# Sums of a graph layer moved to idle buffers, one accumulator made known to a planned order, and the planned lengths set anew

## The chip, the cores and the metric

One core of a Trainium2 chip runs the whole program. The metric is the device time in microseconds (us) of that core; lower is better. PE stands for TensorE (matmuls), DVE for VectorE, ACT for ScalarE, POOL for GpSimd, SP for SyncE, which here issues nearly all DMAs.

## What is computed

The input is x (3327 x 256) and a dense matrix adj (3327 x 3327), of whose entries about 0.5% and the diagonal are not zero. Two layers follow each other, both with a layer norm and a ReLU ahead and a residual after. Layer 0 takes two steps over the graph and over a learned sparse attention; layer 1 attends over the neighbours with four heads.

```python
R = S + eye(N); R = R / R.sum(-1, keepdims=True)        # S is adj
for n in range(2):
    A = top_p_attention(Xa, W1, W2, W3)                 # softmax row, cut to the largest that hold 0.9 of it
    Xf = R @ Xf
    Xa = A @ Xa
    Z = Z + Xf @ U1[n].T + Xa @ U2[n].T
...
e = leaky_relu(s[:, :, None] + d[:, None, :], 0.2)      # layer 1, per head
attn = softmax(where(adj > 0, e, -inf), axis=2)
out = elu(attn @ hp)
```

## The kernel before, in words

N is cut into 26 tiles of 128 nodes (NT = 26, P = 128). All matmuls are float32, each of which the profile shows as two entries.

*How the work is ordered.* The program isn't written in the order in which it runs. Each piece of work is put on record with `plan.put(engine, length, rank, fn, needs=, take=, give=, lag=, hold=)`: the engine, how long the writer thinks it takes (us), a rank, what must be done before, and which named tokens (buffers) it takes and gives back. `Plan.order()` then plays the whole program through with these lengths: whenever an engine is free it takes the ready piece of lowest rank whose tokens are free. `hold` marks a DVE piece as one that stops POOL meanwhile. `plan.issue()` emits the instructions in that order. On the chip every engine runs its own instructions strictly in the order so found, and semaphores see to the true dependences. A length that is off therefore never makes a wrong result; it makes an order that doesn't suit. The tokens exist only in the planner: real buffers are tiles of pools, and a tile that is still in use makes the engine wait whether the planner knew or not.

*Layer 0* has two steps, n = 0 (about 100 to 900 us) and n = 1 (about 900 to 1708 us). In each, 26 rows of three kinds of work interleave:

- Search, per row tile: logits on PE (L882), exponentials on ACT (L893), then a threshold found by rounds: ACT counts over all 3327 columns (L930), POOL (lines 943 to 976; in the last round DVE) works out the next threshold from the count. DVE then takes windows (L985, L990), sorts, chooses, and drops the entries under the threshold (L1042).
- Attention, per row tile: PE transposes the row in groups of four (L1055), ACT copies each group from PSUM (L1060, tiles `et`), PE multiplies (L1067, into `acca`).
- The product with adj, per row tile (class `Full`): SP loads seven pieces of adj (L1088, tiles `at`), PE does 26 matmuls (L1099, into `accf`), ACT copies the result (L1106), DVE adds (L1115, L1121). In step 0 a row's result has its own `accf` tile of 257 columns. In step 1 one tile of [128, 2, 256] serves all rows, and rows use its two halves in turn; the planner has a token for each half (`accf0`, `accf1`).

*Layer 1* (`attend_neighbours`, 1708 to 2177 us) goes over four blocks of 832 target nodes, and in each over 26 source tiles j: a mask from adj on ACT (L1634, L1635), the exponents on DVE in two halves of two heads each (L1646, into an `e` tile of [128, 4, 832]), the product on PE in two halves (L1662), and for every second j the denominators on PE (L1676). The `e` tiles are seven in turn: for j % 7 < 4 one of four tiles of the pool `e` (token "e"), else one of three made from large tiles that layer 0 has left (token "e2"). When a block is done, its sums leave PSUM: ACT copies the numerators (L1724) and the denominators (L1727) to an SBUF tile, which is also one of the pool `e`. From that, for each 128 targets, PE transposes three times (L1746), DVE inverts (L1750), ACT forms both parts of elu (L1758), DVE joins and adds x (L1762, L1763), SP stores. This runs during the next block.

*The verdict.* The fast way holds for inputs in a certain reach. At the end a flag says whether it held: five small DVE operations, then twice a DVE copy, a PE transpose (L1936) and a DVE maximum (L1937), and a last DVE operation (L1938). All engines load the flag and branch past the general way (L1945). These instructions stand after `plan.issue` in the text.

Of the kernel before, what the change touches and what calls it, by code (L numbers as in the profile page):

```python
# [19 lines left out]
P = 128  # L20
# [552 lines left out]
def fast(  # L573
# [59 lines left out]
    with ExitStack() as l0:  # L633
# [215 lines left out]
        plan = Plan(dict(rows=1, mvs=3, pl=2, px=2, acca=1, accf=1, accf0=1, accf1=1, et=3, at=4, y=1, e2=3, mask=2, **BUFS))  # L849
# [227 lines left out]
        class Full:  # L1077


            def __init__(self, n, t):  # L1080
                self.n, self.t, self.at = n, t, {}
                self.src, self.w = (main, D + 1) if n == 0 else (c, D)
                self.bank = f"accf{t % 2}" if n else "accf"
# [6 lines left out]
            def some(self, js):  # L1090
                for j in js:
                    if j == 0 and self.n == 0:
                        self.acc = ps_a.tile([P, D + 1], F32, name="accf")
                    elif j == 0:

                        if self.t == 0:
                            late["accf"] = ps_a.tile([P, 2, D], F32, name="accf")
                        self.acc = late["accf"][:, self.t % 2, :]
                    T.matmul(  # L1099
                        self.acc[:, : self.w], self.at[j // JC][:, j % JC, :], self.src[:, j, : self.w],  # L1100
                        start=(j == 0), stop=(j == NT - 1),
                    )
# [30 lines left out]
        def deviations(lo, hi):  # L1133


            m, held = hi - lo, {}

            def first(k):
                if k == 0:
                    held["mv"] = small.tile([P, 4, 4], F32, name="mvs", bufs=3)  # L1140
                st = small.tile([P, V.BN_STATS_DIM], F32, name="bst", bufs=3)
                V.bn_stats(st, rhs[0][:, lo + k, :])
                V.bn_aggr(held["mv"][:, k, :2], st)

            def rest():
                mv = held["mv"][:, :m]
                GP.tensor_scalar(mv[:, :, 2], mv[:, :, 1], LN_EPS, None, ALU.add)
                GP.tensor_tensor(mv[:, :, 2], mv[:, :, 2], powers[:, 0:1].to_broadcast([P, m]), ALU.pow)
                GP.tensor_tensor(mv[:, :, 3], mv[:, :, 0], mv[:, :, 2], ALU.mult)
                GP.tensor_scalar(mv[:, :, 3], mv[:, :, 3], -1.0, None, ALU.mult)  # L1150

            a = []
            for k in range(m):
                a.append(
                    plan.put("DVE", 0.62, -100.0 + lo + k, first, k, needs=[loads[lo + k], a], take=["mvs"] * (k == 0))
                )
            a = plan.put("POOL", 1.1 + 0.2 * m, -100.0 + lo, rest, needs=[a])
            return {lo + k: (a, held, k, k == m - 1) for k in range(m)}

        def prepare(t, measured):  # L1160
# [36 lines left out]
            a = hs[0][t] = plan.put("ACT", 0.6, r, relu, needs=[ready_], give=["mvs"] * last)  # L1197
            a = plan.put("PE", 0.25, r, turn, needs=[a], take=["pl"])
            a = turned_h[t] = plan.put("DVE", 0.43, r, copy, needs=[a], give=["pl"])
            a = plan.put("PE", 0.5, r, project, needs=[a, weighed], take=["px"])  # L1200
            a = plan.put("ACT", 0.3, r, share, needs=[a], take=["kq"], give=["px"])
# [9 lines left out]
        def project_u(t, rank):  # L1211
            held = {}


            bank = ("acca", "accf")[t % 2] if t > 7 else "px"

            def product():
                ps = held["ps"] = (ps_x if bank == "px" else ps_a).tile([P, 2 * D], F32, name=bank)
                for k in range(2):
                    T.matmul(ps, c[:, t, k * P : (k + 1) * P], u1[:, k, :], start=(k == 0), stop=(k == 1))  # L1220

            a = plan.put("PE", 1.75, rank, product, needs=[turned_h[t], uloads], take=[bank])
            b = plan.put("ACT", 0.37, -2.3, lambda: S.copy(main[:, t, :D], held["ps"][:, :D]), needs=[a])
            e = plan.put("DVE", 0.43, -2.3, lambda: V.tensor_copy(c[:, t, :], held["ps"][:, D:]), needs=[a])
            plan.put("SP", 0.0, -2.6, lambda: None, needs=[b, e], give=[bank], lag=0.0)
            return b, e
# [91 lines left out]
        def finish2(row, done, z, rank):  # L1318
# [67 lines left out]
            a = plan.put("POOL", 0.85, r, deviation, False, needs=[a])  # L1386
            a = plan.put("DVE", 1.6, r, second, needs=[a, x_], take=["mv"], give=["mv"], hold=0.95)
            s_ = plan.put("SP", 0.1, r, store, needs=[a])
            a = plan.put("POOL", 1.1, r, deviation, True, needs=[a])
# [6 lines left out]
            return plan.put("DVE", 0.6, r, scale, needs=[a], give=["f"]), s_  # L1396
# [24 lines left out]
        def search(row, rank, keys, stats_of, fresh):  # L1421
# [4 lines left out]
            for g in range(2):  # L1426

                def logits(g=g):
# [4 lines left out]
                    "PE", 2.0 - 0.8 * g, rank - 2.5, logits, needs=[keys, fresh, a], take=["pl", "pl"] + ["e", "sc"] * (1 - g)  # L1433
# [8 lines left out]
            a = row.pieces["guess"] = plan.put("ACT", 1.0, rank - 2.4, row.guess, needs=[a])  # L1442
            more = plan.put("ACT", 0.85, rank - 2.2, row.density, needs=[a])
# [6 lines left out]
            if EVALS[n] == 3:  # L1450
                a = row.pieces["counted"] = plan.put("ACT", 3.05, rank - 1.4, row.count, 2, AF.Sign, needs=[a])
                a = plan.put("DVE", 2.7, rank - 1.3, row.step, 2, V, needs=[a])
            halves = []
            for h in range(2):
                for part in range(2):
                    a = plan.put(
                        "DVE", 3.2 - 2.0 * part, rank - 1.0, row.window, h, part, needs=[a], take=["y"] * (1 - part),
# [8 lines left out]
            for o in range(4):  # L1466
                a = plan.put("DVE", 1.03, rank - 1.0, row.drop, o, needs=[a], hold=1.0)
                drops.append(a)
# [4 lines left out]
        def attention(row, rank, total, drops, right):  # L1473
            a = None
            for g in range(GROUPS):
# [6 lines left out]
                b = plan.put("ACT", 0.03 + 0.115 * m, rank - 2.6, row.turned, g, needs=[b], take=["et"], give=["px"])  # L1482
# [5 lines left out]
        def full(n, t, rank, right, after):  # L1488
# [7 lines left out]
            for j in range(0, NT, 2):  # L1496
# [3 lines left out]
                    take=[f.bank] * (j == 0) + ["accf"] * (n == 1 and t + j == 0), give=["at"] * last,  # L1500
                )
            a = plan.put(
                "ACT", 0.3, -90.0, f.copy, needs=[a], take=["f"],
                give=[f.bank] + ["accf"] * (n == 1 and t == NT - 1),
# [6 lines left out]
        def attend_neighbours(rows, ends, done, fulls):  # L1511
# [78 lines left out]
            for b in range(4):  # L1590
# [14 lines left out]
                for j in range(NT):  # L1605
# [83 lines left out]
                    else:  # L1689
# [7 lines left out]
                        "DVE", 2.1, rank, exponents, 0, needs=[m_, both[0], ends[j][0], more if mine == "e2" else None,  # L1697
                        logits_done, last_e], take=[mine], hold=2.0,
                    )
                    y_ = plan.put("DVE", 2.1, rank, exponents, 1, needs=[x_, both[1]], give=own, hold=2.0)  # L1700
# [8 lines left out]
                    if len(group) == JG or j == NT - 1:  # L1709
                        for n_, (fn, name) in enumerate(group):  # L1710
                            last_den = plan.put(
                                "PE", 1.42 + 0.2 * (n_ == 0), rank, fn, needs=[last_acc, last_den],
# [7 lines left out]
                def leave(k, q=q):  # L1720
                    if k == 0:
                        q["ot"] = epool.tile([P, NP], F32, name="e")[:, : 3 * W].rearrange("p (k c w) -> p k c w", k=3, c=2)
                    if k < 2:
                        S.copy(q["ot"][:, k], q["acc"][k][:, :, :C])  # L1724
                    else:
                        for c in range(2):
                            S.copy(q["ot"][:, 2, c], q["den"][c][:, :C])  # L1727

                r1 = r0 + 9.0
                first = plan.put("ACT", 0.9, r1, leave, 0, needs=[last_acc], take=["e"], give=["pl"])  # L1730
# [3 lines left out]
                for x0 in range(0, W, P):  # L1734
# [7 lines left out]
                    def turn(m=m, x0=x0, q=q, held=held):  # L1742
                        held["pr"] = ps_x.tile([P, 3, P], F32, name="px")
                        ot = q["ot"].rearrange("p k c w -> p k (c w)")
                        for k in range(3):
                            T.transpose(held["pr"][:m, k, :], ot[:, k, x0 : x0 + m], ident)  # L1746
# [63 lines left out]
                    elif x0 % (4 * P) == 0:  # L1810
                        f_ = plan.put("SP", 0.4, r1, fetch_all, needs=[used_heads[0] if x0 == 0 else [last_e, f_], touched], take=["e"] * (x0 > 0), lag=4.0)
                    a = plan.put(
                        "PE", 0.4, r1 + 0.02, turn, needs=[out_of], take=["px"], give=["e"] * (x0 + P >= W)
# [9 lines left out]
                    a = plan.put("ACT", 2.0, r1, elu, needs=[a], take=["ystage"], give=["px", "mv"])  # L1823
                    a = plan.put("DVE", 1.0, r1, add, needs=[a, f_], give=["f"], hold=0.9)
# [31 lines left out]
        for n in range(STEPS):  # L1856
# [24 lines left out]
            failed.append(plan.put("DVE", 2.2, base + NT, failures, n, needs=[[a for a, _ in found]]))  # L1881
# [41 lines left out]
        plan.issue(tc)  # L1923

        V.tensor_reduce(far, sd.rearrange("p k t h -> p k (t h)"), AX.X, ALU.max, apply_absolute_value=True)
        V.tensor_tensor(far[:, 0:1], far[:, 0:1], far[:, 1:2], ALU.max)
        V.tensor_scalar(far[:, 0:1], far[:, 0:1], REACH, 0.0, ALU.is_le, ALU.is_equal)
        V.tensor_reduce(far[:, 1:2], bad.rearrange("p n t -> p (n t)"), AX.X, ALU.max)
        V.scalar_tensor_tensor(far[:, 0:1], far[:, 1:2], 0.0, far[:, 0:1], ALU.is_gt, ALU.max)

        verdict = const.tile([1, 2], F32, name="verdict")
        for k in range(2):
            r = small.tile([P, D], F32, name="xa", bufs=BUFS["xa"])
            V.tensor_copy(r[:, :1], far[:, 0:1])
            pr = ps_x.tile([1, P], F32, name="px")
            T.transpose(pr, r[:, :1], ident)  # L1936
            V.tensor_reduce(verdict[:, k : k + 1], pr, AX.X, ALU.max)  # L1937
        V.tensor_tensor(again, verdict[:, 0:1], verdict[:, 1:2], ALU.max)  # L1938
# [46 lines left out]
```

## Time and profile before

| what | us |
|---|---|
| median of 3 runs | 2197.55 (2196.28 to 2198.43) |
| the profiled execution | 2193.86 |
| its span in the profile | 2192.1 |
| PE busy in it | 2158.7 |
| DVE busy | 1605.3 |
| ACT busy | 1441.6 |
| POOL busy | 926.6 |
| granted TensorE clock | 0.997 of full |

The page cuts the span in 40 slices of 54.8 us: slices 1 and 2 are the start, about 3 to 16 step 0, 17 to 31 step 1, 32 to 40 layer 1. A digit is the busy share of a slice in tenths. "Busy" of an engine counts the time from an instruction's start to its end; for PE these ends are modelled. The kinds of work that hold PE longest:

| line | what | entries | mean ns of one | busy us |
|---|---|---|---|---|
| L1067 | attention, layer 0 | 2704 | 379 | 618.2 |
| L1099 | product with adj, step 1 | 1352 | 383 | 316.1 |
| L1099 | product with adj, step 0 | 1352 | 381 | 309.8 |
| L1662 | product, layer 1 (one of its groups) | 1024 | 517 | 192.5 |

The entries overlap in time: the mean of one is longer than the step from one start to the next.

### The profile page before, as it was taken

How to read it: one execution, taken by the hardware profiler on the slowest of the kernel's cores; microseconds unless marked ns; L12 is line 12 of the kernel's file. 1: busy time of each engine (PE TensorE's matmuls, PEld its weight loads, DVE VectorE, ACT ScalarE, POOL GpSimd, SP SyncE). 2: the span in 40 equal slices, each digit the busy share in tenths (PEclk: the TensorE clock that was granted, in tenths of full speed). 3: DMA queues.
4: the chain of work that ended last, by engine and by line, in shares of the span. 5: the costliest groups of instructions: out<-in, count | busy, mean ns of one | idle time of the engine just before them, and what ended most of it. 6: DMA issues, size and time to landing. Idle time of an engine off the chain costs nothing. (4 is left out here: it accounts for less than half of the span.)

```text
span 2192.1 us, 35711 instructions
## 1 busy us (share of the span) xinstructions
PE 2158.7 (98%) x11872; PEld 1519.1 (69%) x11872; DVE 1605.3 (73%) x4205; ACT 1441.6 (66%) x2714; POOL 926.6 (42%) x2259
## 2 busy tenths in 40 slices
PE   8999999999999999999999999999999999999997
PEld 6578778778787788777778777878788433333332
DVE  5567666657556571367998888788878898989896
ACT  5786776667666742578888787788673556465553
POOL 5466565546533550265666665656563100000001
PEclk9999999999999999999999999999999999999999
DMA  4012122222222233532222222222124534444341
GB/s 121 21 36 85 48 63 62 64 72 64 57 58 62 72 116 92 154 95 58 63 59 64 59 74 61 75 75 69 56 72 136 157 114 145 119 137 127 110 127 53
DMA packets 192323, 183.74 MB, mean 84 GB/s; under 512 B 15386, under 2 KB 146176, under 8 KB 192128
## 3 DMA queue, kind: packets, MB, share of 16 engines
q1 hardware_dynamic: 191232, 181.15, 28.4%
q8 instruction: 95, 1.56, 0.3%
q14 instruction: 100, 0.82, 0.1%
q10 hardware_dynamic: 896, 0.21, 0.0%
HBM read 164.41 MB, written 15.94 MB: 82 GB/s over the span
## 5 line engine op out<-in xcount | busy, mean ns | idle before, releaser
L1067 PE MATMUL acca<-rhs,et 128*128 128x256 f32 x2704 | 618.2, 379 | 0.1
L930 ACT ACTIVATE junk<-e,sc 128x3327 fp8e5<-128x3327 f32 x182 | 558.8, 3070 | 81.4 <-POOL sc L975 81.0
L1067 PEld LDWEIGHTS acca<-rhs,et 128*128 128x128 f32 x2704 | 498.3, 190 | 61.8 <-issue 1.8
L1099 PE MATMUL accf<-c,at 128*128 128x256 f32 x1352 | 316.1, 383 | 6.3 <-ACT f L1106 5.7
L985 DVE SCALAR_TENSOR_TENSOR y<-e,sc 128x1664 f32<-128x1664 f32 x104 | 204.8, 1969 | 152.6 <-POOL sc L972 150.3
L1099 PE MATMUL accf<-main,at 128*128 128x257 f32 x1352 | 309.8, 381 | 1.5 <-ACT f L1106 1.5
L1099 PEld LDWEIGHTS accf<-c,at 128*128 128x128 f32 x1352 | 249.2, 190 | 54.1 <-issue 10.6
L1099 PEld LDWEIGHTS accf<-main,at 128*128 128x128 f32 x1352 | 251.4, 190 | 46.1 <-issue 8.1
L1060 ACT COPY et<-px 128x512 f32<-128x512 f32 (+1 forms) x364 | 192.6, 553 | 119.5 <-PE acca L1067 62.9
L990 DVE MAX8 cands<-y 128x8 f32<-128x208 f32 x832 | 242.2, 361 | 3.6
L1042 DVE SCALAR_TENSOR_TENSOR e<-e,thr 128x832 f32<-128x832 f32 x208 | 212.9, 1081 | 2.0
L893 ACT ACTIVATE e<-pl 128x1024 f32<-128x1024 f32 x208 | 179.9, 869 | 43.3 <-PE pl L882 43.3
L1635 ACT ACTIVATE et<-at 128x448 bf16<-128x448 f32 (+1 forms) x204 | 112.3, 550 | 131.9 <-DVE e L1646 74.2
L1798 POOL TENSOR_TENSOR qq<-qq 128x256 f32<-128x256 f32 x4 | 3.0, 757 | 461.2 <-ACT qq L1794 461.1
L1055 PE MATMUL px<-ident,e 128*128 128x128 f32 x1352 | 191.9, 274 | 6.0 <-ACT et L1060 3.5
L1055 PEld LDWEIGHTS px<-ident,e 128*128 128x128 f32 x1352 | 160.1, 141 | 50.0 <-issue 13.5
L1662 PE MATMUL pl<-e,main 128*64 128x416 f32 x1024 | 192.5, 517 | 0.3
L882 PE MATMUL pl<-kt,qq 64*128 64x512 f32 (+1 forms) x832 | 173.7, 536 | 0.8 <-ACT e L893 0.8
L1662 PEld LDWEIGHTS pl<-e,main 128*64 128x64 f32 x1024 | 70.9, 137 | 113.3 <-issue 86.4
L1646 DVE SCALAR_TENSOR_TENSOR e<-c,low,et 128x832 f32<-128x832 f32 x128 | 128.6, 1070 | 12.0 <-PE accf L1676 10.4
L882 PEld LDWEIGHTS pl<-kt,qq 64*128 64x128 f32 x832 | 71.5, 186 | 84.4 <-issue 77.3
L1646 DVE SCALAR_TENSOR_TENSOR e<-qq,low,et 128x832 f32<-128x832 f32 x120 | 120.4, 1072 | 6.0 <-PE accf L1676 4.4
(534 smaller groups left out, 3032.3 us busy)
## 6 DMA issues: line engine op xcount, KB each, us to landing
at<-in_adjt_dram SPq DMA_DIRECT2D x414, 256.0 KB
at<-in_adjt_dram SPq DMA_DIRECT2D x102, 192.0 KB
at<-in_adjt_dram SPq DMA_DIRECT2D x52, 128.0 KB
ys<-ystage SPq DMA_DIRECT2D x26, 256.0 KB
rhs<-in_x_dram SPq DMA_DIRECT2D x26, 128.0 KB
ystage<-in_x_dram SPq DMA_DIRECT2D x26, 128.0 KB
base<-ys SPq DMA_DIRECT2D x26, 128.0 KB
x1s<-ystage SPq DMA_DIRECT2D x26, 128.0 KB
```

The source lines that it names most:

```text
L882: T.matmul(pl[:, lo : lo + m], qq[half, self.i, :], kt[half, 512 * k : 512 * k + m], start=True, stop=True,)
L893: S.activation(self.e[:, 1024 * k : 1024 * k + pl.shape[1]], pl, AF.Exp, accum_out=(self.p0, self.p1, self.p2, self.p3)[k],)
L930: S.activation(junk[:, :N], self.e[:, :N], fn, bias=t, scale=-1.0, accum_out=dst, saturate=False)
L985: V.scalar_tensor_tensor(self.y[:, : hi - lo], self.e[:, lo:hi], self.up, self.e[:, lo:hi], ALU.is_lt, ALU.mult, accum_out=(self.h0, self. ...
L990: V.max(self.cands[:, o // PIECE, :], self.y[:, o - lo : min(o + PIECE, hi) - lo])
L1042: V.scalar_tensor_tensor(piece, piece, self.thr[:, o : o + 1], piece, ALU.is_gt, ALU.mult)
L1055: T.transpose(pt[:, k, :], self.e[:, j * P : (j + 1) * P], ident)
L1060: S.copy(self.et[g][:, :m, :], self.pt.pop(g)[:, :m, :])
L1067: T.matmul(self.acc, et[:, j - 4 * g, :], rhs[self.n][:, j, :], start=(j == 0), stop=(j == NT - 1))
L1099: T.matmul(self.acc[:, : self.w], self.at[j // JC][:, j % JC, :], self.src[:, j, : self.w], start=(j == 0), stop=(j == NT - 1),)
L1646: V.scalar_tensor_tensor(held["e"][:, k, :], extra["both"][b % 2][:, k, :], low[:, j, k : k + 1], held["mask"], ALU.max, ALU.mult,)
L1662: T.matmul(q["acc"][a][k * FH : (k + 1) * FH, c, :C], main[:, j, h * FH : (h + 1) * FH], held["e"][:, h, c * C : (c + 1) * C], start=(j == 0),
```

## The change

It has four parts.

(a) The sums of a layer-1 block are copied to a tile `y` (the window tile of layer 0's search, without use in layer 1) and, for the denominators, to the tile `kt` (keys of layer 0), instead of a tile of the pool `e`. The token follows: "y" instead of "e".

(b) In step 1, too, each row has its own `accf` tile, of 256 columns; the pool holds one. The tokens `accf0` and `accf1` are gone: a row's first pair of matmuls takes "accf", its copy gives it back.

(c) Lengths given to the planner are set anew in some thirty places. They add no instruction; they alter the order of the pieces on all engines.

(d) The verdict becomes three planned pieces of rank 92, which lies in the last quarter of layer 1, with one transpose instead of two.

```diff
-        plan = Plan(dict(rows=1, mvs=3, pl=2, px=2, acca=1, accf=1, accf0=1, accf1=1, et=3, at=4, y=1, e2=3, mask=2, **BUFS))
+        plan = Plan(dict(rows=1, mvs=3, pl=2, px=2, acca=1, accf=1, et=3, at=4, y=1, e2=3, mask=2, **BUFS))
...
-                    if j == 0 and self.n == 0:
-                        self.acc = ps_a.tile([P, D + 1], F32, name="accf")
-                    elif j == 0:
-
-                        if self.t == 0:
-                            late["accf"] = ps_a.tile([P, 2, D], F32, name="accf")
-                        self.acc = late["accf"][:, self.t % 2, :]
+                    if j == 0:
+                        self.acc = ps_a.tile([P, self.w], F32, name="accf")
...
-            return plan.put("DVE", 0.6, r, scale, needs=[a], give=["f"]), s_
+            return plan.put("DVE", 0.47, r, scale, needs=[a], give=["f"]), s_
...
-            a = row.pieces["guess"] = plan.put("ACT", 1.0, rank - 2.4, row.guess, needs=[a])
-            more = plan.put("ACT", 0.85, rank - 2.2, row.density, needs=[a])
+            a = row.pieces["guess"] = plan.put("ACT", 1.46, rank - 2.4, row.guess, needs=[a])
+            more = plan.put("ACT", 0.55, rank - 2.2, row.density, needs=[a])
...
-                a = plan.put("DVE", 2.7, rank - 1.3, row.step, 2, V, needs=[a])
+                a = plan.put("DVE", 3.35, rank - 1.3, row.step, 2, V, needs=[a])
...
-                    take=[f.bank] * (j == 0) + ["accf"] * (n == 1 and t + j == 0), give=["at"] * last,
+                    take=["accf"] * (j == 0), give=["at"] * last,
                 )
             a = plan.put(
-                "ACT", 0.3, -90.0, f.copy, needs=[a], take=["f"],
-                give=[f.bank] + ["accf"] * (n == 1 and t == NT - 1),
+                "ACT", 0.35, -90.0, f.copy, needs=[a], take=["f"], give=["accf"],
             )
...
-                        "DVE", 2.1, rank, exponents, 0, needs=[m_, both[0], ends[j][0], more if mine == "e2" else None,
-                        logits_done, last_e], take=[mine], hold=2.0,
+                        "DVE", 2.0, rank, exponents, 0, needs=[m_, both[0], ends[j][0], more if mine == "e2" else None,
+                        logits_done, last_e], take=[mine], hold=1.95,
...
-                        q["ot"] = epool.tile([P, NP], F32, name="e")[:, : 3 * W].rearrange("p (k c w) -> p k c w", k=3, c=2)
+                        q["ot"] = scr.tile([P, 2 * W], F32, name="y").rearrange("p (k w) -> p k w", k=2)
+                        q["ot"] = [q["ot"][:, 0], q["ot"][:, 1]]
                     if k < 2:
-                        S.copy(q["ot"][:, k], q["acc"][k][:, :, :C])
+                        S.copy(q["ot"][k].rearrange("p (c w) -> p c w", c=2), q["acc"][k][:, :, :C])
                     else:
+                        if "den" not in extra:
+                            extra["den"] = wpool.tile([P, 2 * W], F32, name="kt")[:, :W]
+                        q["ot"].append(extra["den"])
                         for c in range(2):
-                            S.copy(q["ot"][:, 2, c], q["den"][c][:, :C])
+                            S.copy(q["ot"][2][:, c * C : (c + 1) * C], q["den"][c][:, :C])
...
-                first = plan.put("ACT", 0.9, r1, leave, 0, needs=[last_acc], take=["e"], give=["pl"])
+                first = plan.put("ACT", 0.9, r1, leave, 0, needs=[last_acc], take=["y"], give=["pl"])
...
-                        "PE", 0.4, r1 + 0.02, turn, needs=[out_of], take=["px"], give=["e"] * (x0 + P >= W)
+                        "PE", 0.4, r1 + 0.02, turn, needs=[out_of], take=["px"], give=["y"] * (x0 + P >= W)
...
-                    a = plan.put("ACT", 2.0, r1, elu, needs=[a], take=["ystage"], give=["px", "mv"])
-                    a = plan.put("DVE", 1.0, r1, add, needs=[a, f_], give=["f"], hold=0.9)
+                    a = plan.put("ACT", 1.6, r1, elu, needs=[a], take=["ystage"], give=["px", "mv"])
+                    a = plan.put("DVE", 0.8, r1, add, needs=[a, f_], give=["f"], hold=0.9)
...
+        verdict = const.tile([1, 2], F32, name="verdict")
+        def judge():
+            V.tensor_reduce(far, sd.rearrange("p k t h -> p k (t h)"), AX.X, ALU.max, apply_absolute_value=True)
...
+        def gather_rows():
+            late["pr"] = ps_x.tile([1, P], F32, name="px")
+            T.transpose(late["pr"], far[:, 0:1], ident)
+        def tell():
+            V.tensor_reduce(verdict[:, 0:1], late["pr"], AX.X, ALU.max)
+            V.tensor_tensor(again, verdict[:, 0:1], verdict[:, 0:1], ALU.max)
+        a = plan.put("DVE", 1.5, 92.0, judge, needs=[[a for a, _ in ends], failed])
+        a = plan.put("PE", 0.15, 92.1, gather_rows, needs=[a], take=["px"])
+        plan.put("DVE", 0.45, 92.2, tell, needs=[a], give=["px"])
         plan.issue(tc)
...
-        for k in range(2):
-            r = small.tile([P, D], F32, name="xa", bufs=BUFS["xa"])
-            V.tensor_copy(r[:, :1], far[:, 0:1])
-            pr = ps_x.tile([1, P], F32, name="px")
-            T.transpose(pr, r[:, :1], ident)
-            V.tensor_reduce(verdict[:, k : k + 1], pr, AX.X, ALU.max)
-        V.tensor_tensor(again, verdict[:, 0:1], verdict[:, 1:2], ALU.max)
```

## The prediction

> **What bounds the kernel now.** I read, in this order, the page's busy times and slices, the list of waits by engine, the timeline at the places that the waits name, and the order of each engine's instructions before and after.
>
> ```profile
> PE 2158.7 (98%) x11872; PEld 1519.1 (69%) x11872; DVE 1605.3 (73%) x4205; ACT 1441.6 (66%) x2714; POOL 926.6 (42%) x2259
> PE   8999999999999999999999999999999999999997
> DVE  5567666657556571367998888788878898989896
> ```
>
> TensorE (PE) is the bound in every stage, and the change leaves its work as it is: the matmuls of the same lines have the same counts in both programs, except for one transpose less at the end. So the most that can be won is the time in which PE stands still. Outside of its first 60 us, PE's visible gaps (times between the end of one entry and the start of the next) sum to 3.5 us in step 0 of layer 0, 11.2 us in step 1 (900 to 1708 us) and under 0.4 us in layer 1. The waits say what those are:
>
> ```profile
> PE accf L1099 <- ACT f L1106: 7.2, 13, 1.1
> ...
> PE px L1055 <- ACT et L1060: 3.5, 2, 3.2
> ...
> PE px L1055 <- DVE e L1042: 1.1, 3, 0.6
> ```
>
> The columns are total us, times, longest. The first line is what part (b) aims at. The timeline around one case (start, length, what; the wait in brackets):
>
> ```profile
> 938.84 0.37 ACT L1106 COPY f<-accf 128x256 f32<-128x256 f32 x1 [2.49 <-PE accf L1099]
> ...
> 939.27 1.99 PE L1099 MATMUL accf<-c,at 128*128 128x256 f32 x8 [0.46 <-ACT f L1106]
> ```
>
> PE went from row t to row t+1 without a pause and did its first 8 matmuls, since row t+1 has its own half of the tile. The copy of row t began only after those (ACT stood idle 2.49 us for PE), and PE then waited for the copy. The start-to-start step of these matmuls is 215 ns; here it is 840, and the step after it 320. There are seven such places, and two with 956: 7 x (0.625 + 0.104) + 2 x (0.741 + 0.104) = 6.8 us; with the gap of 1.1 at the first row (917.6), about 8 us.
>
> Layer 1 looks full on PE and is not. VectorE (DVE) shows waits there:
>
> ```profile
> DVE e L1646 <- PE accf L1676: 14.7, 4, 4.4
> ...
> DVE e L1646 <- ACT e L1724: 3.3, 2, 1.7
> ```
>
> ```profile
> 1853.25 3.01 PE L1662 MATMUL pl<-rhs,main 128*64 128x416 f32 x16
> 1856.10 4.17 PE L1662 MATMUL pl<-e,main 128*64 128x416 f32 x16
> 1860.19 0.91 PE L1676 MATMUL acca<-rhs,qd 128*32 128x416 f32 x8
> ...
> 1863.12 1.27 PE L1662 MATMUL pl<-e,main 128*64 128x416 f32 x6
> ```
>
> The same 16 matmuls took 3.01 us and then 4.17. From 1856.10 to 1863.12 is 7.02 us; the same stretch (product of one j, then its pair's products and sums) takes 5.82 elsewhere. The other two boundaries between column blocks give 7.05 and 7.46. So 1.20 + 1.23 + 1.64 = 4.1 us is lost there, counted as busy. The cause stands 30 us earlier: the sums of a finished block sit in an e tile (line 1724), so the exponents at j=2 and j=3 of the new block wait for a buffer, 18 us in all, so 6.0 per boundary. At j=7 DVE is then 0.5 to 0.9 us behind PE, where it is some us ahead in the rest of a block (DVE needs 3.98 us a j, PE 4.33).
>
> **What the Trainium skill says.** "PSUM — Partial Sum Buffer", Terms: a bank is 2 KiB per partition, and two engines must not be in one bank and quadrant together. Two halves of 256 float32 fill just one bank, so a second half cannot give overlap; the trace agrees with the 2.49 us above. "Trainium Kernel Development and Optimization", Performance Expectations: matmul busy time is a bad measure because matmuls are pipelined; the 4.17 against 3.01 us is this. "TensorE: Matmul & The Clock Gate", Architectural detail: ACT and DVE take their queues strictly in order; the trace agrees in the third rival below. "TensorEngine Tiling (Array Packing)", Key Properties: a change of tiling mode drains TensorE; here the step from L1662 to L1676 is 442 ns against 345, so about 0.1 us a switch.
>
> **The change part by part**, against the profiled execution of 2193.86 us (span 2192.1), which lies 3.69 under the median 2197.55. I carry the difference over to the median.
>
> *Sums to other buffers (a).* The copies of the sums (L1724, L1727) go to the window tile and the old key tile, idle in layer 1. Same copies, same sizes, no DMA. The buffer wait of DVE goes, and in the new DVE order j=0 to j=3 follow each other directly, with the block's epilogue (7 groups of some 1.07 us) from j=4. DVE gets those 6.0 us per boundary back, more than the 0.5 to 0.9 it lacks at j=7. Next late would be DVE itself, but it gains 0.35 us per j. Bounds: -4.1 (all), -1.5 (the epilogue, now in one run, takes the lead back at two boundaries). I take -3.7.
>
> *Accumulator known to the plan (b).* A row change now needs the copy before its first matmul. The plan knows that and can put other PE work there. With nothing there, the wait is about 0.85 us instead of 0.215 (a lone change at the first rows shows 842 ns), so 0.64 + 0.10 = 0.74, the same as a stall now. In the new PE order, three row changes of step 1 are bare (rows 27, 35, 37; nine were before), and five have 0.87 to 1.06 us of cover, the others more. Cover of 1 us hides a copy of 0.37 plus two hand-overs if ACT is free; if a count (L930, 3.07 us) is in front, up to 3 us show. I reckon 3 x 0.74 = 2.2, plus 0.3 at each of ten others at which ACT will be busy, an estimate (a tenth of a count), = 3.0. That is 5.2 instead of 6.8; the 1.1 at the first row stays: -1.6. Bounds: -6 (all covered), +1 (ACT late at more of them).
>
> *Lengths (c).* They add no instruction; they move the order on all engines, and with it each row's DMA issue on SP (`at` loads) and POOL's steps. By the start-to-start steps that are longer than usual, step 1 has 6.7 us of stalls outside the accumulator: 3.4 at 1566.5, 0.8 for one load at 1183, the rest small. Longer plan lengths for guess and the DVE step say later what was in truth later. I take -1.0, bounds -4 and +3 (from nearly none left, to one more like 1566.5). Step 0 and the start: 0, bounds -1 and +1; the trace shows no stall there above 1.1.
>
> *Start of layer 1.* One product piece (4 x 345 ns = 1.4 us) has moved ahead of the last row's adjacency work. It filled the time in which the exponents of j=2 and 3 come after the last row: now PE reaches the second half of j=3 just 0.14 us after DVE (1721.62 against 1721.48). The chain from the last row through copy, finish and four exponents is not shortened. So 1.4 - 0.1 = +1.3; bounds 0 and +1.5.
>
> *Verdict (d).* In PE's order one 128-wide transpose now sits in block 3: 0.11 + two mode switches of 0.1 = +0.3. DVE's pieces (1.5 + 0.45 as planned) stand in front of exponents, but in a block where DVE leads by more than that; if that lead were gone they would cost 2. At the end two transposes and their reductions go. The chain there is this:
>
> ```profile
> 2185.16 0.73 SPq L1805 DMA_DIRECT2D out_dram<-e  x2
> 2185.39 0.27 DVE L1937 TENSOR_REDUCE verdict<-px 1x1 f32<-1x128 f32 x1
> 2185.70 0.15 DVE L1938 TENSOR_TENSOR again<-verdict 1x1 int32<-1x1 f32 x1
> ```
>
> SP issues its last store until 2185.89, the verdict is ready at 2185.85: two chains end together, only one is shortened. I take -0.2; bounds 0 and -0.6.
>
> Sum: -3.7 - 1.6 - 1.0 + 1.3 + 0.3 - 0.2 = -4.9. The profiled execution would be 2189.0, the median 2192.65, said as 2192.7.
>
> **The rivals.** A difference under 0.2% (4.4 us: 2193.15 to 2201.95) is about what a measurement of this kernel cannot tell from none.
>
> *Step 1 is cleaned up as a whole.* The stalls of step 1 are 6.8 + 1.1 + 6.7 = 14.6 us; my sum takes 2.6 of it. If a plan with true lengths removes half, 7.3, the median is 2197.55 - 4.9 - 4.7 = 2188.0. For it: six fewer bare row changes, and each stall comes from an order that was planned with lengths off by up to 0.65 us. Against: the waits for POOL come from steps whose lengths (3.8 and 4.7) were not changed.
>
> *The wait only moves.* Row changes now wait openly for ACT, which is in a count 3 us long for much of the time; step 1 gains nothing, and only half of the boundaries' gain comes (-2.1), less 1.3 + 0.3 - 0.2: -0.7, so 2196.8. For it: ACT is busy 7 to 8 tenths in most slices of step 1. The weaker form, that the change does not do what it says, belongs here: the sums leave the e tiles but the exponents wait for the sums' matmuls (L1676) of the buffers they reuse.
>
> *Slower.* ACT runs in order. The plan may put a count ahead of the copies that PE needs, when its POOL step is late:
>
> ```profile
> 1562.85 3.07 ACT L930 ACTIVATE junk<-e,sc 128x3327 fp8e5<-128x3327 f32 x1 [5.39 <-POOL sc L975]
> ...
> 1566.53 1.09 PE L1055 MATMUL px<-ident,e 128*128 128x128 f32 x8 [3.23 <-ACT et L1060]
> ```
>
> The count waited 5.39 us for POOL, the copies (L1060) stood behind it, PE stood 3.23. Each such place costs 3.2. It happens once now; two more would eat my gain, three make it slower: -4.9 + 3 x 3.2 = +4.7, so 2202.3. For it: the whole order is new, and POOL's lengths are not retuned. Against: once in 52 rows now.
>
> **How the numbers follow.** My sum 2192.7 (own range 2189.5 to 2196): 0.46, of which 0.25 under 2193.15. Step 1 cleaned up, 2188.0: 0.23. The wait moves, 2196.8: 0.17. Slower, 2202.3: 0.14. So faster 0.25 + 0.23 = 0.48, within 0.21 + 0.17 = 0.38, slower 0.14. The range 2186.5 to 2199 leaves out the slower case and the far end of the cleaned-up one.
>
> **What would show it.** Right: no DVE wait for PE at L1639 (the exponents' line after) at a block's j=2 and 3, and 5.8 us stretches at j=7; the wait of L1099 for the copy at 4 to 6 us, before a row's first matmul; a PE gap of about 1 us some 13 us after the last adjacency row. Wrong: waits at L1099 above 8 us, more than one PE gap of 3 us behind a count, or the 7 us stretches still there.

## The result and the profile after

| | us |
|---|---|
| before, median of 12 runs | 2197.49 (2195.89 to 2198.89) |
| after, median of 12 runs | 2198.52 (2196.15 to 2200.91) |
| ratio after to before | 1.0005, 95% interval 0.9997 to 1.0012 |
| forecast | 2192.7 (2186.5 to 2199.0) |
| profiled execution after, and its span | 2199.53, 2197.6 |

The change makes no difference that can be measured, where 4.9 us less were forecast. The measured time lies inside the stated range, 0.5 us from its upper end. The profiled execution of before (2193.86) was a fast one by chance: all of its timed runs lie above it, by 0.7 us or more over the whole study. So the two spans, 5.5 us apart, exaggerate; what follows is read by stage.

The table cuts each profile at four points of PE's work: the first product with adj of step 0, the first of step 1, the first product of block 1 of layer 1, and the last product. The "last product" is the start of its last entry. Two programs that are equal up to a point differ there only by chance.

| profile | start | step 0 | step 1 and block 0 | blocks 1 to 3 | rest |
|---|---|---|---|---|---|
| before | 95.4 | 822.2 | 905.9 | 350.0 | 18.5 |
| after | 98.6 | 824.2 | 910.2 | 346.0 | 18.6 |

Blocks 1 to 3 won 4.0 us. Step 1 with block 0 lost 4.3, step 0 lost 2.0, of which an estimated 1.7 come from a stretch of half clock (last section). The start's 3.2 us aren't the change's: in the profiles of the twelve experiments it took 96.5 to 99.2 us, in six of them with the order of before there.

The page and the waits of after (PE's first, then DVE's in layer 1), whose L1093 is before's L1099, L1100 is L1106, L1639 is L1646, L1655 is L1662, L1669 is L1676:

```profile
PE 2160.0 (98%) x11871; PEld 1520.6 (69%) x11871; DVE 1607.1 (73%) x4202; ACT 1442.7 (66%) x2714; POOL 935.7 (43%) x2259
DVE  5566676547565572277979879788878799999895
```

```profile
PE accf L1093 <- ACT f L1100: 8.6, 11, 2.0
...
PE px L1055 <- ACT et L1060: 2.7, 3, 1.6
PE acca L1067 <- ACT et L1060: 2.2, 2, 2.0
PE px L1232 <- ACT xa L1073: 2.0, 1, 2.0
...
PE px L1055 <- DVE e L1042: 0.8, 2, 0.5
```

```profile
DVE e L1639 <- PE accf L1669: 2.9, 2, 2.2
```

The reader is to see two things. DVE's wait for a buffer fell from 14.7 to 2.9 us. And PE's waits for ACT didn't fall, but changed their places: the accumulator's line grew from 7.2 to 8.6, and two lines are new (L1067 for a copy, L1232 for `xa`).

What was won, at j=7 of block 1 (timeline of PE in after):

```profile
1862.51 3.01 PE L1655 MATMUL pl<-rhs,main 128*64 128x416 f32 x16
1865.36 2.96 PE L1655 MATMUL pl<-e,main 128*64 128x416 f32 x16
1868.25 0.91 PE L1669 MATMUL acca<-rhs,qd 128*32 128x416 f32 x8
...
1871.18 2.32 PE L1655 MATMUL pl<-e,main 128*64 128x416 f32 x12
```

The sixteen matmuls that took 4.17 us take 2.96, and the stretch is 1871.18 - 1865.36 = 5.82 us instead of 7.02.

What was lost. A row change in step 1 (ACT and PE in after): the copy stands behind a count, the count behind POOL, and PE's first matmul of the row behind the copy.

```profile
1204.92 3.07 ACT L930 ACTIVATE junk<-e,sc 128x3327 fp8e5<-128x3327 f32 x1 [2.15 <-POOL sc L975]
...
1207.98 0.35 ACT L1100 COPY f<-accf 128x256 f32<-128x256 f32 x1
...
1208.39 2.86 PE L1093 MATMUL accf<-c,at 128*128 128x256 f32 x12 [1.44 <-ACT f L1100]
```

The end of layer 0 (SP, ACT and PE in after): ACT has the first mask of layer 1 (into `kt`) ahead of the last copy of an attention row. The mask waits 4.59 us for its load, and PE 2.00 us for the copy behind it.

```profile
1665.16 5.78 SPq L1604 DMA_DIRECT2D kt<-in_adjt_dram  x4
...
1673.88 0.90 ACT L1611 ACTIVATE kt<-kt 128x832 f32<-128x832 f32 x1 [4.59 <-DMA kt<-in_adjt_dram]
...
1675.61 0.35 ACT L1060 COPY et<-px 128x256 f32<-128x256 f32 x1
...
1676.01 1.13 PE L1067 MATMUL acca<-rhs,et 128*128 128x256 f32 x4 [2.00 <-ACT et L1060]
```

And the start of layer 1 (PE in after): 32 entries, for which twice the 2.85 us from start to start of 16 would be 5.7 us, take 7.18 us, since DVE's exponents for j=2 and j=3 come late.

```profile
1724.83 7.18 PE L1655 MATMUL pl<-e,main 128*64 128x416 f32 x32
```

### The profile page after: what moved, and what is told of

Same layout as the page of the kernel before. It is cut to its first block, busy times and chain, and to the rows that moved or that the text cites. A ratio compares the mean times of both kernels' runs of the same rounds, so it can differ in the third digit from the quotient of the medians.

```text
span 2197.6 us, 35753 instructions
## 1 busy us (share of the span) xinstructions
PE 2160.0 (98%) x11871; PEld 1520.6 (69%) x11871; DVE 1607.1 (73%) x4202; ACT 1442.7 (66%) x2714; POOL 935.7 (43%) x2259
## 4 chain that ended last, share of the span: by engine, by line
PE 42%; POOL 5%; ACT 4%; issue 1%; DVE 1%; DMA 0%; SPq 0%; DVEq 0%; POOLq 0%; ACTq 0%
PE pl L1655 13%; PE accf L1093 8%; PE acca L1067 8%; PE acca L1669 4%; PE accf L1669 3%; ACT junk L930 3%; PE px L1055 2%; PE pl L882 2%; POOL sc L943 1%; PE px L1359 1%; PE px L1742 0%; POOL sc L968 0%; DMA kt<-in_adjt_dram 0%; DVE e L1639 0%; ACT et L1060 0%
## 5 line engine op out<-in xcount | busy, mean ns | idle before, releaser
L1067 PE MATMUL acca<-rhs,et 128*128 128x256 f32 x2704 | 618.4, 379 | 2.3 <-ACT et L1060 2.2
L1067 PEld LDWEIGHTS acca<-rhs,et 128*128 128x128 f32 x2704 | 498.2, 190 | 66.0 <-ACT et L1060 3.5
L1093 PE MATMUL accf<-c,at 128*128 128x256 f32 x1352 | 315.2, 382 | 7.9 <-ACT f L1100 7.9
L1093 PE MATMUL accf<-main,at 128*128 128x257 f32 x1352 | 309.5, 380 | 0.7 <-ACT f L1100 0.7
L1093 PEld LDWEIGHTS accf<-c,at 128*128 128x128 f32 x1352 | 249.5, 190 | 53.4 <-ACT f L1100 12.6
L1093 PEld LDWEIGHTS accf<-main,at 128*128 128x128 f32 x1352 | 251.6, 190 | 44.3 <-issue 8.3
L1055 PE MATMUL px<-ident,e 128*128 128x128 f32 x1352 | 191.7, 274 | 3.8 <-ACT et L1060 2.7
L1055 PEld LDWEIGHTS px<-ident,e 128*128 128x128 f32 x1352 | 160.0, 141 | 46.8 <-issue 10.9
L1655 PE MATMUL pl<-e,main 128*64 128x416 f32 x1024 | 190.3, 517 | 0.1
L1655 PEld LDWEIGHTS pl<-e,main 128*64 128x64 f32 x1024 | 70.6, 137 | 110.7 <-issue 90.8
L1639 DVE SCALAR_TENSOR_TENSOR e<-c,low,et 128x832 f32<-128x832 f32 x128 | 128.7, 1071 | 5.7 <-issue 3.2
L1627 ACT ACTIVATE at<-at 128x448 f32<-128x448 f32 (+1 forms) x204 | 110.4, 541 | 31.0 <-DMA at<-in_adjt_dram 30.8
```

The costliest lines, as they stand in the source:

```text
L1055: T.transpose(pt[:, k, :], self.e[:, j * P : (j + 1) * P], ident)
L1067: T.matmul(self.acc, et[:, j - 4 * g, :], rhs[self.n][:, j, :], start=(j == 0), stop=(j == NT - 1))
L1093: T.matmul(self.acc[:, : self.w], self.at[j // JC][:, j % JC, :], self.src[:, j, : self.w], start=(j == 0), stop=(j == NT - 1),)
L1655: T.matmul(q["acc"][a][k * FH : (k + 1) * FH, c, :C], main[:, j, h * FH : (h + 1) * FH], held["e"][:, h, c * C : (c + 1) * C], start=(j == 0),
```

## The experiments

Each kernel was timed in five rounds beside the kernel before, whose medians in the three groups were 2197.38, 2197.45 and 2197.79. The theory at the outset: (a) is worth its 4 us, and the new order of layer 0 gives them back. The rival: what the parts bring adds up, and the two profiles differ by chance.

**Each part alone.** `a_sums_only`: the diff's part (a), nothing else.

```diff
-                        q["ot"] = epool.tile([P, NP], F32, name="e")[:, : 3 * W].rearrange("p (k c w) -> p k c w", k=3, c=2)
+                        q["ot"] = scr.tile([P, 2 * W], F32, name="y").rearrange("p (k w) -> p k w", k=2)
...
+                            extra["den"] = wpool.tile([P, 2 * W], F32, name="kt")[:, :W]
...
-                first = plan.put("ACT", 0.9, r1, leave, 0, needs=[last_acc], take=["e"], give=["pl"])
+                first = plan.put("ACT", 0.9, r1, leave, 0, needs=[last_acc], take=["y"], give=["pl"])
```

> The kernel before with part (a) alone: the sums go to the idle tiles; the order of layer 0 and of the first block of layer 1 stays. Theory: part (a) is worth what it was forecast to be, and it is given back elsewhere. The three stretches of 7.0 to 7.5 us at j=7 become 5.8, so 4.0 us less: about 2193.5, a ratio near 0.998. Rival: the exponents are then held by another buffer, or the gain shows only in one profile: 2197.5, ratio 1.000.

Measured: 2192.9, ratio 0.9980 (0.9973 to 0.9988). Blocks 1 to 3 took 345.8 us; step 0 (822.2) and step 1 with block 0 (905.9) were those of before. DVE's wait in layer 1:

```profile
DVE e L1646 <- PE accf L1676: 0.6, 1, 0.6
```

So (a) brings what the prediction gave it, and does so alone.

`b_accumulator_only`: part (b), with the copy's length left at 0.3.

> The kernel before with part (b) alone (one accumulator, known to the plan, the copy's length left at 0.3). Theory: a row change that waits openly for ACT costs more in sum than the half-tile stall, since ACT is often in a count of 3 us: step 1's accumulator waits go from 6.1 to about 7.9 us, the time to about 2199. Rival, as in the prediction's sum: they go to about 4.5 us, time 2196.

Measured: 2204.1, ratio 1.0029 (1.0017 to 1.0041). The sign of the theory holds, its size doesn't: 6.7 us lost, not 1.5. Step 1 and block 0 took 914.9 us. Accumulator waits alone don't explain it (7.3 us from 900 to 1730 us in the list of waits, against 5.7). There are also two stalls of 3.4 and 3.1 us on ACT's copies. The first has a counterpart of 3.2 us in before (the place near 1566 us that the prediction shows), the second is new. After both, PE ran at half the clock for some us (last section), which it didn't in the profile of before.

`c_lengths_only`: part (c), with two halves and the sums in `e` as before (and the copy's length left at 0.3).

```diff
-            a = row.pieces["guess"] = plan.put("ACT", 1.0, rank - 2.4, row.guess, needs=[a])
+            a = row.pieces["guess"] = plan.put("ACT", 1.46, rank - 2.4, row.guess, needs=[a])
...
-                    a = plan.put("ACT", 2.0, r1, elu, needs=[a], take=["ystage"], give=["px", "mv"])
+                    a = plan.put("ACT", 1.6, r1, elu, needs=[a], take=["ystage"], give=["px", "mv"])
...
```

> The kernel before with part (c) alone, all the new lengths. Theory: the new order costs about 2 us in step 0 (one gap of 2 us near 131 us, one of 0.7 near 118) and 1.4 us at the start of layer 1: about 2200. Rival: the start of the program is later as well, by 3 us as in the one profile of the change: about 2203. Rival, as in the prediction's sum: the lengths are worth -1.0: 2196.5.

Measured: 2192.24, ratio 0.9979 (0.9973 to 0.9986). Here my theory was wrong: the lengths as a whole win. The gap near 130 us came as expected (step 0: 825.9 us against 822.2), but step 1 and block 0 took 903.9, and blocks 1 to 3 took 346.0 although the sums still sit in an `e` tile. At j=7 of block 1:

```profile
1859.90 2.96 PE L1662 MATMUL pl<-e,main 128*64 128x416 f32 x16
...
1865.73 3.71 PE L1662 MATMUL pl<-e,main 128*64 128x416 f32 x20
```

5.83 us. DVE still waits for the buffer (4.5 us in three places), but the exponents are now ordered so that it is 0.1 to 1.2 us ahead at j=7 instead of 0.5 to 0.9 behind. A lead of any size is enough: where DVE leads by 8 us and more at j=7, as in after, PE takes the same 5.8 us.

`d_verdict_only`: part (d).

> The kernel before with part (d) alone: the verdict is planned inside the last block. Theory: +0.3 us in the last block from one transpose and two changes of tiling mode, nothing at the end, since SP's own chain ends there: 2197.8. Rival: the end gets shorter by 0.2 to 0.6 us and the block no longer: 2197.1. The two can hardly be told apart by the times, but by the profile.

Measured: 2196.69, ratio 0.9996 (0.9987 to 1.0004): no difference that can be told. The rest after the last product is 18.2 against 18.5 us.

The four parts alone sum to -4.5 + 6.7 - 5.1 - 0.7 = -3.6; together they gave +1.0. So they don't add up, and the next three runs say where.

**Parts left out.** `all_but_sums`: the changed kernel with the sums in an `e` tile again.

> The changed kernel with part (a) undone: the sums go to an e tile again. Theory: the new lengths of layer 1 alone order a block's start so that DVE isn't behind at j=7, so (a) and (c) are two ways to the same 4 us and (a) adds nothing to (c): 2198.5 (+-1.5), blocks 1 to 3 at about 116.5 us each. Rival: the gains of the parts add up, 2198.5 + 4.5 = 2203.

Measured: 2199.72, ratio 1.0009 (1.0001 to 1.0017). Blocks 1 to 3 took 346.8 us. Undoing (a) costs 1.2 us in the medians, hardly clear of the scatter, and not 4.5: (a) and the lengths of layer 1 are two ways to the same 4 us. What (a) adds is a thicker lead: without it DVE was 0.3 us behind again at j=7 of block 3, and that stretch took 6.25 us.

`all_but_accumulator`: the changed kernel with the tile of two halves and its tokens.

> The changed kernel with part (b) undone: step 1 has the tile of two halves again, with its two tokens. Theory: (b) costs 6 to 7 us with the new lengths, too, as it did alone: 2192. Rival: with true lengths the plan makes good use of the token, (b) costs nothing: 2198. Rival: all gains add up (a -4.5, c -5.1, d -0.7): 2187.

Measured: 2192.77, ratio 0.9980 (0.9974 to 0.9987). So (b) costs 5.75 us (2198.52 - 2192.77) in the changed kernel too. `layer1_parts_only`: (a), (d) and layer 1's lengths on the kernel before.

> The kernel before with (a), (d) and the lengths of layer 1 alone: layer 0 keeps its order. Theory: the boundaries' 4 us once, and (d) -0.5: 2193. Rival: (a) and the lengths of layer 1 add up: 2189. Rival: the lengths of layer 1 delay its start by 1.4 us as in the changed kernel: 2194.5.

Measured: 2193.06, ratio 0.9978 (0.9969 to 0.9987); blocks 1 to 3 346.0. This is (a) alone within 0.2 us: the gain comes once.

**What in (b) costs.** (b) is a tile and a token. `tile_only` changes the tile and leaves the planner its two tokens, so the order is before's:

```diff
-                    if j == 0 and self.n == 0:
-                        self.acc = ps_a.tile([P, D + 1], F32, name="accf")
-                    elif j == 0:
...
+                    if j == 0:
+                        self.acc = ps_a.tile([P, self.w], F32, name="accf")
```

> The kernel before with the tile of part (b) alone: one accumulator tile per row, while the planner keeps its two tokens, so that the order stays as before. Theory: an open wait before a row's first matmul costs about what the stall after its first eight did (0.64 against 0.63 us a place), so 2197.5 to 2199; what (b) costs is its new order. Rival: the tile itself is the cost, since at a bare row change ACT may be in a count: 2202 to 2204.

Measured: 2215.19, ratio 1.0079 (1.0066 to 1.0093). The rival was right in kind, not in size: the tile costs 17.4 us in the order of before, where it gave 4 to 6. Its waits, and one row change (ACT, then PE):

```profile
PE accf L1094 <- ACT f L1101: 18.4, 16, 3.0
```

```profile
1197.80 3.06 ACT L930 ACTIVATE junk<-e,sc 128x3327 fp8e5<-128x3327 f32 x1
...
1200.85 0.35 ACT L1101 COPY f<-accf 128x256 f32<-128x256 f32 x1
...
1201.25 3.30 PE L1094 MATMUL accf<-c,at 128*128 128x256 f32 x8 [3.02 <-ACT f L1101]
```

At five bare row changes the copy had no count ahead on ACT and PE stood 0.46 us; at four it had one and PE stood 2.4 to 3.0 us. After three of these four, PE ran at half clock for 3.0 to 3.4 us more. With two halves, the first matmuls of the new row (eight entries, 1.7 us, in the case that the prediction shows) and what the plan put after them run under that count. That is what the second half was for.

`token_only` leaves the two halves and gives the planner one token.

```diff
-                self.bank = f"accf{t % 2}" if n else "accf"
+                self.bank = "accf"
...
+                    take=["accf"] * (j == 0), give=["at"] * last,
```

> The kernel before with the token of part (b) alone: the planner sees one accumulator, while the tile keeps its two halves. Theory: the order that the token brings puts the first masks of layer 1 ahead of the copies of an attention row, and the masks wait for their load; so most of the 6.7 us of (b) are here: 2201 to 2204. Rival: the order is as good as the other: 2197.

Measured: 2204.71, ratio 1.0029 (1.0018 to 1.0040): as much as all of (b). Once the plan knows the accumulator, the tile makes no difference that these runs can tell (2204.1 with one accumulator, 2204.7 with two halves); the order that the plan then makes does. Its largest stall:

```profile
1675.45 0.90 ACT L1618 ACTIVATE kt<-kt 128x832 f32<-128x832 f32 x1 [5.94 <-DMA kt<-in_adjt_dram]
...
1679.31 2.07 PE L1067 MATMUL acca<-rhs,et 128*128 128x256 f32 x4 [4.23 <-ACT et L1060]
```

In all four profiles with (b)'s token and the load's old lag, the mask waits 4.6 to 6.7 us for its load; in none of the eight with the two tokens.

**The number behind it.** The plan holds that this load lands 4 us after its issue; in after, the mask started 8.7 us after (1673.88 - 1665.16). In the order of before it was nearly so: the mask ran 4.95 us after the first issue and didn't wait for the load. The four issues took 2.16 us on SP there and 5.78 in after; why the load is slower in the new order was not taken apart.

```profile
1664.02 2.16 SPq L1611 DMA_DIRECT2D kt<-in_adjt_dram  x4
...
1668.97 0.90 ACT L1618 ACTIVATE kt<-kt 128x832 f32<-128x832 f32 x1
```

`changed_with_true_lag` tells the plan 10 us:

```diff
-loads, own = plan.put("SP", 0.2, rank, load_first, needs=[opened[0]], lag=4.0), []
+loads, own = plan.put("SP", 0.2, rank, load_first, needs=[opened[0]], lag=10.0), []
```

> The changed kernel with one number altered: the planner is told that the first load of layer 1 takes 10 us to land instead of 4, so that ACT has the last copy of the attention row ahead of the masks that wait for this load. Theory: the PE gap of 2.0 to 4.1 us near 1677 us and the low clock after it go, some 3 us: 2195.5. Rival: the gap was hidden elsewhere or the layer starts later by as much: 2198.5.

Measured: 2195.09, ratio 0.9990 (0.9983 to 0.9996), so 3.4 us under the changed kernel. In the two profiles step 1 with block 0 differs by 1.1 us only (909.1 against 910.2), in part since the one of this run has a stretch of half clock in step 1 and that of after has none there; the size of the gain rests on the medians. ACT's order at that place is now this, and PE waits 0.2 us there:

```profile
1670.42 0.37 ACT L1060 COPY et<-px 128x256 f32<-128x256 f32 x1 [1.36 <-PE acca L1067]
1674.75 0.47 ACT L1073 ACTIVATE xa<-acca,sc 128x256 f32<-128x256 f32 x1 [3.95 <-PE acca L1067]
1675.12 0.89 ACT L1611 ACTIVATE kt<-kt 128x832 f32<-128x832 f32 x1
```

`all_but_accumulator_and_turned_length`: without (b), and one length of (c) set back.

```diff
-                b = plan.put("ACT", 0.06 + 0.105 * m, rank - 2.6, row.turned, g, needs=[b], take=["et"], give=["px"])
+                b = plan.put("ACT", 0.03 + 0.115 * m, rank - 2.6, row.turned, g, needs=[b], take=["et"], give=["px"])
```

> The changed kernel with part (b) undone and one length set back, that of the copy of transposed groups (0.03 + 0.115 m instead of 0.06 + 0.105 m). In its order the scaling of the first attention row (L1073) stands ahead of a copy (L809) that waits 2.9 us for DVE near 130 us. Theory: the gap of 2.0 us there and the low clock after it go, 3 us less than the kernel without (b): 2189. Rival: the order changes elsewhere by as much: 2192 or more.

Measured: 2189.09, ratio 0.9965 (0.9952 to 0.9979), the best of all, better than both kernels. The time is what was expected, the reason only in part. Step 0 took 822.6 instead of 823.7, as the gap near 130 us made room for one of 1.4 us at 135.5; 1.3 us more are in step 1 with block 0, where this order has no stall of 1.5 us or more. (The medians differ by 3.7, the two profiles by 0.2 in all: that of `all_but_accumulator`, 2188.67, is 4.1 us under its median, has no half clock outside the start and the end, and began 2.6 us earlier. In the order here a stall of 2.0 and one of 2.3 us are gone, which in other profiles were at times followed by half clock; that this is the rest of the 3.7 is likely, not shown.) PE's waits from 900 to 1730 us:

```profile
PE accf L1099 <- ACT f L1106: 5.3, 8, 1.2
PE px L1055 <- DVE e L1042: 1.2, 1, 1.2
PE px L1055 <- ACT et L1060: 0.5, 1, 0.5
```

`changed_with_true_lag_and_turned_length`: both repairs, (b) kept.

> The changed kernel with both repairs of its order: the load's 10 us and the old length of the turned copies. Theory: both gaps go (near 130 us and near 1677 us), and what is left of (b)'s cost is the start of layer 1 and its accumulator waits: 2192, still above the 2189.1 of the kernel without (b). Rival: (b) is no cost in itself once no queue stands behind a load: 2189 or less.

Measured: 2191.6, ratio 0.9973 (0.9963 to 0.9983). Repaired, the changed kernel beats the one before, but (b) still costs some 2.5 us against the same without it: step 1 and block 0 take 905.7 against 900.8 us in the profiles (step 0, 821.0 against 822.6, gives some of it back). From 900 to 1730 us PE's list has 8.5 us of accumulator waits against 5.3, and 1.9 us of L1055 waiting for copies against 0.5: together 4.6 of the 4.9 us. The two largest are row changes with a count ahead of the copy, 1.74 us at row 32 and 1.96 at row 35.

## Why the prediction was right or wrong

The time came near the upper end of the range, and the gain that was forecast did not come. Without (b) one of nearly that size did: the other terms together were forecast at -3.3, and the change without (b) gave -4.7 (`all_but_accumulator`). (b) was forecast at -1.6 and cost 5.75. That alone is 7.4 us, more than the 5.9 by which the whole was off. That the time still lies in the range is owed to the range's width and to what the other parts gave beyond their terms.

*Sums (a), -3.7.* Right: -4.0 in the stage, -4.5 by the medians. It was not said that the lengths of layer 1 reach the same by themselves; in the whole change (a) adds 0.8 us in the stage.

*Accumulator (b), -1.6, bounds -6 and +1.* This is the step that failed: +6.7 alone, +5.75 in the whole, outside its bounds. Two terms were off. The row changes without the first: 5.2 us were reckoned, 7.9 measured in after, by the steps from start to start. The three changes called bare gave 0.63, 1.60 and 0.63 instead of 0.74 each, and five of those said to have cover gave 5.0 instead of the 3.0 for ten (2.1 at row 32 and 1.2 at row 29), since a count was in front. Behind this stands the reading that a second half in the same bank "cannot give overlap": the copy and the matmuls indeed don't overlap, but matmuls of the next row ran while the copy waited for its turn, and `tile_only` shows what that was worth. The second term was missing: the token alters the whole order of step 1, and the prediction priced only the row changes in it. The mask ahead of a copy (2.0 to 4.2 us of PE) is in ACT's order of the changed program; the prediction compared PE's order row by row, not what stands ahead on ACT.

*Lengths (c), -1.0 for step 1, 0 for step 0.* Step 1 with block 0 gained 2.0 alone, step 0 lost 0.2 to 3.7 in the five profiles with all of (c) (the bounds said 1); in three of them half clock followed the stall near 130 us. In step 0 one piece changed its place on ACT: `xa` (L1073) now stands behind a copy that waits 2.86 us for DVE, and PE 2.04 for `xa`. That is again an in-order queue behind a wait.

*Start of layer 1, +1.3.* Right in kind, 2.2 measured (PE's steps into L1655 in this stage). It comes with the order at the end of layer 0 that (b) and (c) make together: 0.8 with the lag of 10 us, under 0.1 with both repairs, 0 without (b).

*Verdict, +0.3 and -0.2.* Too small to be told by these runs.

*The rivals.* The time, 2198.5, is nearest to "the wait only moves" (2196.8), and waits did move to other places on ACT. But that case had half of the boundaries' gain lost, and all of it came. The case "slower" named the mechanism that decided, ACT in order with something late in front, with a POOL step as the late one. So it was at the row changes 29, 32 and 35, where the count ahead of the copy had waited 1.1 to 2.2 us for POOL; in the other places it was a load and DVE. "Step 1 as a whole", 2188.0, is approached only without (b): 2192.8, and 2189.1 with one length set back as well. Of the signs named for being wrong, one came, accumulator waits above 8 us (8.6); no gap of 3 us and no 7 us stretch at j=7 did.

*What stays open.* Why the plan's order with one token puts counts ahead of the copies in the rest of step 1: 2.5 us remain by the medians when the two stalls are repaired. Why the first load of layer 1 lands later in the new order. Part (d) was not resolved.

## What to carry to other kernels

A planner's list of lengths is a claim about every queue. When one token or length changes, look at all engines' new order for an instruction that waits for a load or a slow engine and stands ahead of what the bound engine needs; the row changes that the edit is about are the smaller part. Two edits that remove the same lateness don't add: ask of each gain whether the consumer already has a lead. And a second buffer half whose copy seems to stall anyway may still be hiding a much longer wait.

## What the runs showed of the hardware

A PE stall can cost more than its length, and not always. The same program part with the same stall near 1566 us (3.23 and 3.24 us) was followed by full clock in the profile of before and by half clock in that of `layer1_parts_only`. The columns are the stretch, its length, busy time and instructions of PE, PEld, DVE, ACT and POOL, then the granted clock, DMA share and GB/s; first before, then `layer1_parts_only`:

```profile
1566.00:1570.00 4.00, 3.47 (x24) 3.25 (x25) 3.47 (x15) 3.29 (x12) 0.41 (x1) 1.00 0.02 6
1570.00:1572.00 2.00, 2.00 (x11) 1.75 (x10) 1.97 (x5) 2.00 (x4) 0.00 (x0) 1.00 0.70 164
```

```profile
1570.00:1572.00 2.00, 1.96 (x9) 1.96 (x10) 1.67 (x10) 0.74 (x2) 0.00 (x0) 0.50 0.03 8
1572.00:1574.00 2.00, 2.00 (x8) 1.53 (x7) 1.87 (x4) 1.85 (x6) 0.00 (x0) 0.50 0.02 4
```

At half clock an entry of L1099 steps 427 ns instead of 215. The clock records of the 14 profiles have 16 such stretches between the start and the end, each behind a stall of PE; PE worked 3.0 to 5.9 us in them, so that each added 1.5 to 3.0 us (an estimate: half of that time). One stands in step 0 of after, from 132 to 135 us. Of the stalls, none under 1.9 us was followed by half clock, 12 of 23 between 1.9 and 3.3 us were, and all four above 3.4 us.

The Trainium skill, "TensorE: Matmul & The Clock Gate", What's actually happening, says that the clock halves after an idle window of about 3.4 us, and that the window runs freely, so that the moment differs between runs. The second agrees with the two profiles above; the first is too mild for this kernel: in `changed_with_true_lag` a stall of 1.97 us that ended at 1206.56 us was followed by a clock of 0.50 (1208 to 1210 us), while one of 1.96 us at the same row change in `changed_with_true_lag_and_turned_length` was not.

Two readings of this study lean on that. The start: from 10 to 30 us the mean granted clock was 0.91 in before and 0.83 in after, that is about 3.4 us more at half clock, an estimated 1.7 of the 3.2 us between the two starts. And the spread of the runs: the 114 timed runs of before in the three groups took 2198.8 us on average where the granted clock of the whole run was 0.995 (24 runs), 2197.3 at 0.996 (60) 2196.4 at 0.997 (26) and 2196.1 at 0.998 (4). The slower runs have the lower clock; that it is the whole cause of the spread is not shown.
